# Three moves in the order of a codebook-convolution kernel: layer 3's bias product, the second chunk's weights, and the overflow count

## The chip, the cores and the metric

The kernel runs on one core of one Trainium2 chip. The metric is the device time of one execution in microseconds (us). The core has five engines that run their own instruction queues in order and wait for each other through semaphores: TensorE (PE in the profile; its weight loads are PEld), VectorE (DVE), ScalarE (ACT), GpSimd (POOL) and SyncE (SP), which here issues nearly all DMA transfers.

## The reference, cut to what matters

The input x is 32 images of 1024 channels and 14 x 14 pixels. Two blocks follow each other. The first one is a bottleneck of three "table" convolutions, each followed by a batch normalisation:

```python
def _amm(patches, centroids, lut, inv_temp):
    v = patches.reshape(B, ncb, sub, H * W).transpose(0, 3, 1, 2)
    scores = 2.0 * einsum('blcs,cks->blck', v, centroids) - sum(centroids * centroids, -1)
    attn = softmax(scores * inv_temp, axis=-1)
    out = einsum('blck,cko->blo', attn, lut)
    ...
out = relu(_bn(_amm(x, c1_centroids, c1_lut)))          # 1024 -> 256
out = relu(_bn(_amm(_extract3x3(out), c2_centroids, c2_lut)))  # 256 -> 256
out = _bn(_amm(out, c3_centroids, c3_lut))              # 256 -> 1024
x = x + relu(out + identity)
```

In words: the channels are cut into groups, each group of a pixel is scored against 16 centroids, a softmax over those 16 gives weights, and the output is the weighted sum of rows of a table. The second block is a linear attention with a depthwise convolution; the change doesn't touch it, and it is called stage 4 below.

## The kernel before, in words

**Stages.** The function `layers` runs the three table convolutions one after the other, then stage 4 follows. In a score product, 128 partitions hold 8 groups of 16 centroids. The softmax over 16 neighbours on the partition axis is done in five steps: ACT takes the exponentials out of PSUM (L568, with a bias for each centroid), DVE transposes in 32 x 32 blocks (L580, tile `tt`), POOL adds the two halves in layers 1 and 2 (L583), DVE sums and takes reciprocals (L599, L601) and transposes the reciprocals back (L611, tile `r`), and POOL multiplies (L618). Then SP spreads some rows to other partitions by small DMAs: where the last of the 16 weights would stand, the kernel puts a row of another tile (L713, L716 in layers 1 and 2; `spread3` and `double3`, L1139 to L1143, in layer 3), since the 16 weights add up to one.

**Layers 1 and 2** are run by `units`: 16 pairs of images times 8 blocks of channels are 128 units, numbered by i. In step i it issues the scores of unit i + 4, the first transpose of unit i + 3, the softmax of unit i + 2, the callback `side(i)`, and the table products of unit i (L734, "the products" below). `side2` is the callback of layer 2. At i = 60 it prepares layer 3: `score_biases` squares and sums the centroids on DVE into a scratch tile `croom`, which is taken from the same two-buffer pool and tag as `r`; `score_matrices` writes the score matrix `cw`; and then `biases()` multiplies on PE (L397, tile `pb`) and finishes on DVE (L401, L402, L406) into `cbias`.

**Layer 3** works on 14 chunks of 448 pixels, with two blocks of channels each, so that (k, b) names a softmax. The prologue does both of chunk 0 and the scores of (1, 0). `first_chunk` makes the eight outputs of chunk 0: outputs 0 to 2 together, then output 3, then 4 to 7 (`whole`, `halves`: L1275 in the profile; `out` copies by ACT at L1298 and takes statistics on DVE at L1257). Three PSUM banks plus one hold the outputs, so that output 4 needs the bank of output 0, and so on. `softmax_steps(k, b, t)` returns four steps: first transpose; sums; back (transpose, multiply, spread); and the sum for the overflow test, an ACT instruction (L622). Chunks 1 to 13 are made by `group(k, 0)` and `group(k, 1)`, which use a Strassen-like scheme with 7 products of halves instead of 8; it needs sums of table blocks (`weight_sums` on POOL, L1198 to L1200; `weight_differences` on DVE, L1206) and sums of softmax halves (`first_sum` on POOL, L1213; `other_sums` on DVE and POOL, L1219 to L1221). The products are at L1358.

**The overflow test.** Exponentials are taken without subtracting the maximum. `overflow` (L629 to L638) compares the sums with 1e36 on DVE (L632, L633), counts with a 1-column product on PE (L635), writes an integer (L637) and loads it into a register of all five engines (L638, `TENSOR_LOAD`). `layers` returns that register, and a branch at L1466 repeats the layers in an exact form if it is positive, which doesn't happen with these inputs. The test stands before the last chunk (k = 13).

**What sets the order.** Inside `layers` the schedule is written by hand: each engine runs its instructions in the order of the program. Only stage 4 has a planner.

Of the kernel before, what the change touches and what calls it, by code (L numbers as in the profile page):

```python
# [12 lines left out]
ALU = mybir.AluOpType  # L13
# [4 lines left out]
P = 128  # L18
# [131 lines left out]
def conv_preact_kernel(ctx: ExitStack, tc: tile.TileContext, a: dict, out: bass.AP):  # L150
    nc = tc.nc
# [347 lines left out]
    def layers(exact, early=None):  # L499
# [20 lines left out]
        parts = {}  # L520
# [35 lines left out]
        def scores(n):  # L556
            return ps_sc.tile([P, 512], F32, tag="sc", name="sc")[:, :n]
# [71 lines left out]
        def overflow(pool):  # L629

            good = pool.tile([P, 1], F32, tag="good", name="good")
            nc.vector.tensor_scalar(sums, sums, 1e36, None, ALU.is_le)  # L632
            nc.vector.tensor_reduce(good, sums, AX.X, ALU.min)  # L633
            pf = scores(1)[:1]
            nc.tensor.matmul(pf, good, ones[:, :1], start=True, stop=True)  # L635
            bad = pool.tile([1, 1], mybir.dt.int32, tag="bad", name="bad")
            nc.vector.tensor_scalar(bad, pf, -1.0, float(P), ALU.mult, ALU.add)  # L637
            return nc.values_load(bad[0:1, 0:1], min_val=0, max_val=P)  # L638

        def add_up(layer, n):  # L640
            if not exact:
# [318 lines left out]
        with ExitStack() as s:  # L960
# [77 lines left out]
            def side2(i):  # L1038

                for b in range(4, 8):  # L1040
                    if i == max(b - 7, -ahead):
                        luts2[b][2]()
                    if i == max(b - 4, 0):
                        luts2[b][4]()
                if i == max(-2, -ahead):
                    luts2[4][3]()
                p = {1: 1}.get(i + ahead, (i + ahead + 9) / 8)
                if p in range(1, NP):
                    for h in range(2):
                        store_pair(int(p), h)  # L1050
                if i == 60:
                    bias3, biases = score_biases(ps_tr, big, st, 3, raw[3], P, 2, mask8, 4)
                    parts[3] = score_matrices(big, 3, "", raw[3], mask8), bias3
                    biases()
                next_lut3(i - 8 * (NP - 1) - 1)

            def next_lut3(b):
# [25 lines left out]
        with ExitStack() as s:  # L1083
# [3 lines left out]
            again = None  # L1087
# [17 lines left out]
            def score3(k, b, parts=None):  # L1105
                v = chunk(k, b)
                scs = []
                for j in range(4):
                    sc = scores(NC)
                    r = slice(32 * j, 32 * j + 32)  # L1110
                    nc.tensor.matmul(
                        sc, w3[r, b, :], v[r], start=True, stop=True
                    )
                    scs.append(sc)
                t = sf.tile([P, 4, NC], F32, tag="t", name="t")
                if parts is None:
                    exponentials(t, scs, bias3[:, 4 * b : 4 * b + 4])
                    return t
                for v in (slice(0, 2), slice(2, 4)):
                    parts.append(  # L1120
                        lambda v=v: exponentials(
                            t[:, v], scs[v], bias3[:, 4 * b : 4 * b + 4][:, v]
                        )
                    )
                return t
# [67 lines left out]
            def weight_sums():  # L1193

                for g in range(3):
                    a11, a21 = luts[1 + g][:, :512], luts[1 + g][:, 512:]
                    a12, a22 = luts[4 + g][:, :512], luts[4 + g][:, 512:]
                    nc.gpsimd.tensor_tensor(s1[:, g], a21, a22, ALU.add)  # L1198
                    nc.gpsimd.tensor_tensor(s2[:, g], s1[:, g], a11, ALU.subtract)
                    nc.gpsimd.tensor_tensor(s4[:, g], a12, s2[:, g], ALU.subtract)  # L1200
# [7 lines left out]
            def first_sum(k):  # L1208
                x = sums3[k] = [
                    xs.tile([P, 3, H], F32, tag=f"x{n}", name=f"x{n}") for n in (1, 2, 4)  # L1210
                ]
                b1 = tiles3[k][0][:, 1:4]
                nc.gpsimd.tensor_tensor(x[0], b1[:, :, right], b1[:, :, left], ALU.subtract)  # L1213
# [9 lines left out]
            def softmax_steps(k, b, t):  # L1223


                u = 2 * k + b

                def spread():
                    tiles3.setdefault(k, []).append(t)
                    rows3[k] = rows3.get(k, []) + split3(t)  # L1230
                    spread3(rows3[k], range(4 * b + (b == 0), 4 * b + 4))
                    if b:
                        double3(rows3[k][0])

                if exact:

                    def whole():
                        softmax(st, u, t, *token_major(st, t))
                        spread()

                    return [whole] + 3 * [lambda: None]
                kept = {}

                def turn():
                    kept["t"] = token_major(st, t)

                def sums():
                    kept["back"], kept["total"] = softmax(st, u, t, *kept["t"], later=True)

                def back():  # L1250
                    kept["back"]()
                    spread()

                return [turn, sums, back, lambda: kept["total"]()]
# [9 lines left out]
            def first_chunk():  # L1264


                rows = rows3[0]
                pos = {}

                def bank(m):  # L1270
                    pool, tag = (ps_tr, "tr") if m % 4 == 3 else (ps_po, "po")
                    pos[m] = pool.tile([P, 512], F32, tag=tag, name="po3")[:, :NC]

                def product(m, g, r=slice(0, P), start=False, stop=False):
                    nc.tensor.matmul(  # L1275
                        pos[m],
                        luts[g][r, m * P : (m + 1) * P],
                        rows[g][r],
                        start=start,
                        stop=stop,  # L1280
                    )

                def whole(m):
                    for g in range(1, CT):
                        product(m, g, start=m == 4 and g == 1, stop=m > 4 and g == 7)

                def halves(m0):
                    for m in (m0, m0 + 1):
                        if m not in pos:
                            bank(m)  # L1290
                        r = slice(64 * (m - m0), 64 * (m - m0) + 64)
                        product(m, 0, r, start=m > 4, stop=m < 5)

                def out(m):
                    if m % 2 == 0:
                        pos["o"] = output()
                    o = pos["o"]
                    nc.scalar.copy(o[:, m % 2], pos[m])  # L1298
                    stats(m, o[:, m % 2], 0)
                    if m % 2:  # L1300
                        nc.sync.dma_start(o3d[:, m - 1 : m + 1, :NC], o)
                    if m in (4, 5):
                        relu3(2, m - 4)

                for m in range(3):
                    bank(m)
                for g in range(1, CT):
                    for m in range(3):
                        product(m, g, start=g == 1)
                bank(3)  # L1310
                for g in range(1, CT):
                    product(3, g, start=g == 1)
                halves(0)
                halves(2)
                out(0)
                for f in softmax_steps(1, 0, nxt):
                    f()
                first_sum(1)
                weight_sums()
                t = score3(1, 1)  # L1320
                out(1)
                bank(4)
                whole(4)
                halves(4)
                halves(6)
                for m in (2, 3):
                    out(m)
                for f in softmax_steps(1, 1, t):
                    f()
                out(4)  # L1330
                for m in range(5, 8):
                    whole(m)
                    if m == 7:
                        weight_differences()
                        other_sums(1)
                    out(m)

            first_chunk()
# [106 lines left out]
                pending.extend(steps[3:])  # L1445

            for k in range(1, NCH):
                if k + 1 == NCH and not exact:
                    add_up(2, 2 * NCH)
                    again = overflow(once)  # L1450
                if early:
                    early.pop(0)(scores)
                for n in range(2):
                    group(k, n)
            bn_final(once, None, 3, range(CT), sc3, bi3, mv3)
        act.close()
        return again
# [802 lines left out]
```

## Time and profile before

| what | value |
|---|---|
| time, median of 3 runs (lowest to highest) | 3439.27 us (3438.05 to 3441.15) |
| the profiled execution's own time | 3446.09 us |
| its span, first to last instruction | 3444.3 us |
| busy share PE / DVE / POOL / ACT | 98% / 85% / 74% / 49% |
| mean granted TensorE clock | 0.990 |
| layer 2's products run from 867 to 1641 us | L734, second half |
| first chunk of layer 3 | 1659.7 to 1709 us |
| groups (1, 0) to (13, 1) | 1709 to 2291 us |
| stage 4 | 2299 us to the end |

A line of a timeline gives start, duration, engine, source line, operation and tile, and in brackets how long the engine had been idle before it and what ended that. A float32 product appears as two matmuls. The granted clock is the share of full speed that TensorE was given in a window. Idle time of an engine that isn't the limit costs nothing.

### The profile page before, as it was taken

What the parts mean: (1) busy time and instruction counts of PE and PEld (TensorE: products, weight loads), DVE (VectorE), ACT (ScalarE), POOL (GpSimd) and SP (SyncE); (2) the same over time, 40 slices, a digit from 0 to 9 for tenths busy, and PEclk for the clock granted to TensorE, in tenths of its full rate; (3) what the DMA queues carried; (4) which work ended last, traced back from release to release, by engine and by line L of the source; (5) the groups of instructions that cost most, each with busy time, mean ns of one, the idle gap of its engine ahead of it and who ended that gap; (6) DMA issues with size and microseconds to landing.
All of it is one profiled execution on the core that took longest, in us unless ns stands there. A gap on an engine that the chain in (4) does not pass through costs nothing. (4 is left out here: it accounts for less than half of the span.)

```text
span 3444.3 us, 54933 instructions
## 1 busy us (share of the span) xinstructions
PE 3368.4 (98%) x19217; PEld 2088.5 (61%) x19217; DVE 2938.9 (85%) x4621; ACT 1671.0 (49%) x3843; POOL 2538.4 (74%) x1558
## 2 busy tenths in 40 slices
PE   8999999998999999999999999979999999999999
PEld 4555555554455445545488888866666666666665
DVE  7999999997888888888576666646999999999996
ACT  4555555554444434443311111118676767676765
POOL 5999999996888988898322222218888888888887
PEclk9999999999999999999999999989999999999999
DMA  3110111103434444443131111131233332333221
GB/s 117 46 48 28 46 46 47 30 24 113 134 109 128 123 114 109 127 123 98 33 91 38 49 49 49 47 130 41 69 90 87 87 87 81 87 87 91 79 76 48
DMA packets 242229, 267.44 MB, mean 78 GB/s; under 512 B 32812, under 2 KB 239700, under 8 KB 241944
## 3 DMA queue, kind: packets, MB, share of 16 engines
q1 hardware_dynamic: 241248, 263.52, 26.3%
q8 instruction: 155, 2.54, 0.3%
q14 instruction: 130, 1.06, 0.1%
q10 hardware_dynamic: 696, 0.31, 0.0%
HBM read 171.01 MB, written 77.09 MB: 72 GB/s over the span
## 5 line engine op out<-in xcount | busy, mean ns | idle before, releaser
L618 POOL TENSOR_TENSOR t<-t,r 128x1568 f32<-128x1568 f32 (+3 forms) x288 | 961.5, 3339 | 531.5 <-issue 201.1
L734 PE MATMUL po<-t,lut 128*128 128x392 f32 x3840 | 1334.6, 500 | 2.5 <-DMA t<-spare 2.5
L734 PEld LDWEIGHTS po<-t,lut 128*128 128x128 f32 x3840 | 711.9, 190 | 603.8 <-issue 83.2
L1770 PE MATMUL mm<-y,lut 128*128 128x392 f32 x2048 | 710.4, 493 | 0.1
L580 DVE STREAM_TRANSPOSE tt<-t 128x1568 f32<-128x1568 f32 (+1 forms) x284 | 517.8, 1823 | 153.4 <-ACT t L568 149.1
L568 ACT ACTIVATE t<-sc,cbias 128x392 f32<-128x392 f32 (+1 forms) x624 | 322.4, 598 | 554.5 <-PE sc L897 191.2
L1992 DVE SCALAR_TENSOR_TENSOR pa<-y,lepe_w,pa 128x406 f32<-128x406 f32 x900 | 537.9, 638 | 3.6 <-PE pa L1974 0.3
L611 DVE STREAM_TRANSPOSE r<-rc 128x1568 f32<-128x1568 f32 (+1 forms) x284 | 520.9, 1834 | 10.4
L1770 PEld LDWEIGHTS mm<-y,lut 128*128 128x128 f32 x2048 | 370.4, 188 | 243.1 <-issue 6.1
L583 POOL TENSOR_TENSOR tt<-tt 128x784 f32<-128x784 f32 x256 | 470.6, 1838 | 30.5 <-DVE tt L580 25.9
L568 ACT ACTIVATE t<-sc,room 128x392 f32<-128x392 f32 x512 | 259.1, 589 | 410.2 <-issue 180.1
L1358 PE MATMUL po<-t,lut 128*128 128x224 f32 (+2 forms) x1352 | 314.8, 416 | 1.3 <-DMA o3d<-o 1.3
L599 DVE TENSOR_REDUCE sm<-tt 128x98 f32<-128x784 f32 (+1 forms) x284 | 293.6, 1034 | 1.1 <-POOL tt L583 0.8
L1358 PEld LDWEIGHTS po<-t,lut 128*128 128x128 f32 (+1 forms) x1352 | 234.7, 190 | 64.5 <-issue 61.8
L601 DVE RECIPROCAL rc<-sm 128x98 f32<-128x98 f32 (+1 forms) x284 | 220.2, 775 | 9.8
L622 ACT ACTIVATE sm<-sm 128x98 f32<-128x98 f32 (+1 forms) x284 | 85.5, 301 | 150.5 <-DVE rc L601 150.5
L1623 ACT ACTIVATE w<-x,tb,gn_a 128x196 f32<-128x196 f32 x248 | 128.3, 517 | 53.8 <-DMA qr<-o3d 29.3
L1814 POOL TENSOR_TENSOR kr<-k,cosq 128x784 f32<-128x784 f32 x64 | 104.3, 1629 | 63.5 <-DVE k L1791 36.7
L1955 POOL TENSOR_TENSOR qr<-qr,zb 128x784 f32<-128x784 f32 x64 | 117.9, 1854 | 39.2 <-DMA zb<-zd 31.5
L1779 ACT ACTIVATE e<-mm,kbd 128x392 f32<-128x392 f32 x128 | 74.5, 582 | 145.4 <-PE mm L1770 145.4
L1782 ACT ACTIVATE e<-e 128x392 f32<-128x392 f32 x256 | 134.9, 527 | 2.1
L1736 ACT ACTIVATE y<-x,gb,ga 128x196 f32<-128x196 f32 x256 | 125.3, 544 | 12.1 <-POOL gb L1699 12.1
(215 smaller groups left out, 4613.1 us busy)
## 6 DMA issues: line engine op xcount, KB each, us to landing
patch<-h1d SPq DMA_DIRECT2D x383, 108.5 KB
x<-in_x_dram SPq DMA_DIRECT2D x32, 784.0 KB
o3d<-o SPq DMA_DIRECT2D x56, 448.0 KB
x<-in_x_dram SPq DMA_DIRECT2D x64, 392.0 KB
out_dram<-x SPq DMA_DIRECT2D x64, 392.0 KB
o<-o3d SPq DMA_DIRECT2D x62, 392.0 KB
h1d<-pad SPq DMA_DIRECT2D x96, 225.0 KB
patch<-h1d SPq DMA_DIRECT2D x383, 54.2 KB
```

Of the source, the lines that this page charges most:

```text
L568: nc.scalar.activation(t[:, j, : sc.shape[1]], sc, AF.Identity if exact else AF.Exp, bias=bias[:, j : j + 1],)
L580: nc.vector.transpose(tt, tf)
L583: nc.gpsimd.tensor_tensor(tv[:, :, :8], tv[:, :, :8], tv[:, :, 8:], ALU.add)
L599: nc.vector.tensor_reduce(sm, tv, AX.X, ALU.add)
L601: nc.vector.reciprocal(rc, sm)
L611: nc.vector.transpose(r, bc(rc, 2, KC))
L618: nc.gpsimd.tensor_tensor(v[:, c], v[:, c], r[:, c], ALU.mult)
L734: nc.tensor.matmul(po[h], luts[b][:, j, h * P : (h + 1) * P], ts[u % len(ts)][:, j, :N2], start=(b == 0 and j == j0), stop=(b == 7 and j = ...
L1358: nc.tensor.matmul(dst, w, x, start=start, stop=stop)
L1770: nc.tensor.matmul(pv(), w[kt][:, m0 : m0 + P], ywin(p, first + kt), start=(kt == 0), stop=(kt == 3),)
L1782: nc.scalar.activation(e(), e(), AF.Exp, scale=-1.0)
L1992: nc.vector.scalar_tensor_tensor(acc, neighbours(p, c, offset(k)), lw[:, c, k : k + 1], acc, ALU.mult, ALU.add,)
```

## The change

Three moves; no arithmetic is added or removed.

1. `biases()` of layer 3 is called four units later, at i = 64, while the DVE work on its operands stays at i = 60. The scratch tile `croom` is therefore held four units longer.
2. In `first_chunk`, the softmax of (1, 0) and `first_sum(1)` are issued at the start; the scores of (1, 1) go between the products of outputs 0 to 2 and those of output 3; the softmax of (1, 1) and then `weight_sums` follow ahead of the first `out`; and `other_sums(1)` moves ahead of `out(4)`.
3. `overflow` returns a function. The comparison stays ahead of the last chunk; the count on PE and the integer on DVE come behind `group(13, 0)`, and the register loads behind `group(13, 1)`, which is ahead of the final normalisation `bn_final`.

```diff
+            def count():
+                pf = scores(1)[:1]
+                nc.tensor.matmul(pf, good, ones[:, :1], start=True, stop=True)
+                bad = pool.tile([1, 1], mybir.dt.int32, tag="bad", name="bad")
+                nc.vector.tensor_scalar(bad, pf, -1.0, float(P), ALU.mult, ALU.add)
+                return lambda: nc.values_load(bad[0:1, 0:1], min_val=0, max_val=P)
+
+            return count
...
                     parts[3] = score_matrices(big, 3, "", raw[3], mask8), bias3
-                    biases()
+                    parts["biases3"] = biases
+                if i == 64:
+                    parts["biases3"]()
...
                 for m in range(3):
                     bank(m)
+                for f in softmax_steps(1, 0, nxt):
+                    f()
+                first_sum(1)
                 for g in range(1, CT):
                     for m in range(3):
                         product(m, g, start=g == 1)
+                t = score3(1, 1)
                 bank(3)
                 for g in range(1, CT):
                     product(3, g, start=g == 1)
+                for f in softmax_steps(1, 1, t):
+                    f()
+                weight_sums()
                 halves(0)
                 halves(2)
                 out(0)
-                for f in softmax_steps(1, 0, nxt):
-                    f()
-                first_sum(1)
-                weight_sums()
-                t = score3(1, 1)
                 out(1)
...
                 for m in (2, 3):
                     out(m)
-                for f in softmax_steps(1, 1, t):
-                    f()
+                other_sums(1)
                 out(4)
...
                         weight_differences()
-                        other_sums(1)
...
             for k in range(1, NCH):
+                check = None
                 if k + 1 == NCH and not exact:
                     add_up(2, 2 * NCH)
-                    again = overflow(once)
+                    check = overflow(once)
                 if early:
                     early.pop(0)(scores)
-                for n in range(2):
-                    group(k, n)
+                group(k, 0)
+                if check:
+                    check = check()
+                group(k, 1)
+                if check:
+                    again = check()
```

More of the change, by code (lines that the diff above doesn't have):

```diff
@@ L633, in overflow @@
             nc.vector.tensor_reduce(good, sums, AX.X, ALU.min)
[L634 to L638, printed above, removed]
+            def count():
[5 more added lines that the diff above has]
+            return count
         def add_up(layer, n):
```

## The prediction

> **What bounds the kernel now.** First the page's busy shares:
>
> ```profile
> PE 3368.4 (98%) x19217; PEld 2088.5 (61%) x19217; DVE 2938.9 (85%) x4621; ACT 1671.0 (49%) x3843; POOL 2538.4 (74%) x1558
> ```
>
> PE is the limit, so only PE's gaps and slow stretches are worth anything. The second view is the waits of PE, asked for the three places that the change touches:
>
> ```profile
> PE po L1358 <- DVE x L1219: 5.6, 1, 5.6
> PE pb L397 <- DMA patch<-h1d: 5.5, 1, 5.5
> ...
> PE sc L635 <- DVE good L633: 2.3, 1, 2.3
> ...
> PE po L1358 <- DMA o3d<-o: 1.3, 1, 1.3
> ...
> PE po L1275 <- ACT o L1298: 1.1, 1, 1.1
> ```
>
> They sum to 15.8 us. The row of L397 names a DMA, but the timeline shows whom PE waited for: L397 needs DVE's L388 (1234.63, 0.29 long), which stood behind an L344 of 3.18 us. The products of unit 60 then began at 1235.56.
>
> ```profile
> 1230.80 3.49 POOL L618 TENSOR_TENSOR t<-t,r 128x1568 f32<-128x1568 f32 x1 [1.00 <-ACT t L568]
> ...
> 1231.13 3.18 DVE L344 TENSOR_SCALAR cmean3b<-cmean3b,cinvt3b 128x2 f32<-128x2 f32 x1
> ...
> 1234.98 0.79 PE L397 MATMUL pb<-croom 128*128 128x128 f32 x2 [5.53 <-DMA patch<-h1d]
> ```
>
> The third view, busy time in three stretches (PE, weight loads, DVE, ACT, POOL, then granted clock, DMA share, GB/s), shows what a gap costs afterwards: the granted clock is 0.51 to 0.64 after each long gap.
>
> ```profile
> 1235.00:1242.00 7.00, 7.00 (x30) 3.86 (x46) 6.69 (x11) 0.00 (x0) 1.83 (x1) 0.64 0.48 129
> 1720.30:1724.80 4.50, 4.46 (x12) 4.06 (x13) 4.48 (x3) 0.00 (x0) 1.45 (x1) 0.51 0.60 207
> 2247.40:2251.20 3.80, 3.80 (x13) 3.54 (x14) 0.00 (x0) 0.35 (x1) 0.00 (x0) 0.61 0.00 0
> ```
>
> **Move 1, the bias product.** Score groups, one a unit (L1027), follow each other by 6.34 us (1215.83, 1222.17, 1228.51), by 5.00 where a unit has 12 products instead of 16 (1204.49 to 1209.49). Unit 60 has 12, so the scores behind 1228.51 were due at 1233.51; they came at 1241.83: 8.3 us lost, 6.2 waiting and 2.1 at half clock. The matmul itself still runs at i = 64: 0.4 (from 1234.97 to the next weight load at 1235.35).
>
> Where does the stall go? DVE still spends 1230.6 to 1236.0 on L382 to L356; only L401, L402 and L406 (0.29 + 0.29 + 0.17) leave. So DVE's next transpose (L580, unit 64) starts at 1236.0, though its input was there at 1231.7 (L568 from 1229.64, 2.02 long): DVE is 4.3 us late. How much lead is there? Unit 61's multiply ends at 1228.01, its small DMA is issued by 1228.64 and lands some 1.4 later (the same DMA of 1236.45 moved its bytes until 1238.4), at 1230.0; undisturbed, its products would start at 1234.4. Lead 4.4 against lateness 4.3: a knife edge. DVE catches up slowly, because `croom` keeps one of the two buffers of `r`: each L611 must now wait for the L618 before it. That hand-over is 1.81 + 0.1 + 3.52 + 0.1 = 5.6 us against a mean unit of (3 x 6.34 + 5.00)/4 = 6.0. Followed through by these rows, operands reach PE at 1247.0 for unit 63 (due 1247.1), 1252.8 for 64 (1253.8), 1258.2 for 65 (1258.8), 1263.8 for 66 (1265.1).
>
> Then a rule enters. L406 now falls at about 1260, within a POOL multiply (1258.4 to 1261.9); before, POOL was idle and it took 0.17. [...] The L344 above is that case: it ended at 1234.31, POOL's L618 at 1234.29, and its twin took 0.23 without POOL. By L406's own row (0.17) unit 67 is about 0.5 us early and nothing is lost; by the rule L406 takes 2.0, unit 67's operands land at 1272.9 against 1271.5, and PE loses 1.4. The L344 rows decide for me: I take 1.5 (between 0 and 3.5, the longest multiply). Gain 8.3 - 0.4 - 1.5 = **6.4** (4.4 to 7.9).
>
> **Move 2, the first chunk.** Here POOL multiplied (1, 1) only at 1712.36, behind nine weight sums; the spread landed at 1719.4:
>
> ```profile
> 1712.33 2.43 PE L1358 MATMUL po<-x,s 128*128 128x224 f32 x12
> 1712.36 3.97 POOL L618 TENSOR_TENSOR t<-t,r 128x1792 f32<-128x1792 f32 x1
> ...
> 1719.43 0.86 DVE L1219 TENSOR_TENSOR x<-t,x 128x672 f32<-128x672 f32 x1 [9.50 <-DMA t<-t]
> ...
> 1720.34 4.68 PE L1358 MATMUL po<-x,s 128*128 128x224 f32 x12 [5.58 <-DVE x L1219]
> ```
>
> The new order, by the same rows. DVE, idle from 1662.1, does (1, 0): 2.03 + 2.02 + 0.85 + 2.04, until 1669.2; POOL multiplies until 1673.3, SP spreads, `first_sum` ends at 1678.3. PE makes 21 products at 0.75 (1659.7 to 1675.5), then the (1, 1) scores; ACT's exponentials run 1677.0 to 1679.2, DVE until 1686.3, POOL until 1690.4; the spread (landing 3.1 behind its first issue, as at 1716.36 to 1719.43) is there at 1693.5, x2 and x4 by about 1696, the nine sums (1.3 each) by 1702, or 1705 if they are held at 1.7 each, as when L1206 ran. Group (1, 0) wants the sums from 1711.8 and x2 at 1714.4: everything is early, and the 5.6 us and the half clock behind it (12 matmuls in 4.3 against 2.3 for the twelve before them: 2.0) go.
>
> What is queued behind? On ACT, `out(0)` now stands behind the overflow sum of (1, 1), which waits for the reciprocals (1684.3). So `out(0)` copies until 1685.4, and output 4 needs its bank: PE, free at 1684.1, waits 1.4. The additional change of row count costs 0.46 (weight loads at 1680.11 and 1680.95, instead of a pitch of 0.375). Against this, the present 2.2 us stall in `halves` disappears (1689.08 to 1693.01 is 3.93; the same work took 1.71 at 1680.95). Together 0.3 gained. On SP the first two output stores slip behind the spreads to about 1697; their buffers are reused at 1711. The thirteen loads for stage 4 begin at about 1710 rather than 1722.6 and last 12, still ahead of the spread of (2, 0), some 20 us into the group. On DVE x2's wait for the spread now stands ahead of the statistics of output 4, which come later than 1693.5 anyway. POOL's queue ends with L1220 after the sums, at 1704 to 1707; its result is wanted some 11 us into the group. Gain **7.9** (6.5 to 9.6: no wait for `out(0)` at the top).
>
> **Move 3, the overflow count.** PE's row behind the count:
>
> ```profile
> 2247.38 3.98 PE L1358 MATMUL po<-t,lut 128*128 128x224 f32 x12 [1.34 <-DMA o3d<-o]
> ```
>
> and, from the rows of one line (minimum, median and maximum duration in ns, then first and last start):
>
> ```profile
> L638 DVEq TENSOR_LOAD <-bad x1: 750/750/750, 2246.5 to 2246.5; - x1
> ```
>
> PE finished group (12, 1) at 2243.6; the second set of group (13, 0) began at 2251.19: 7.6 us for work that takes 2.4 in group (12, 0) (2200.76 to 2203.14). So 5.2 are lost: a gap of 3.8 and 1.4 of half clock. (The wait named a DMA is the register load: 0.75 from 2246.4.) Afterwards the count costs PE two changes of shape (0.46 each, nearest row) and its passes, 1.1 (0.2 to 1.5). `bad` on DVE finds the count done. The loads wait for semaphore values long reached; ACT, POOL and PE have slack there, and SP's stores come first. On DVE the load stands between the last statistics (end 2293.5) and `bn_final`, which stage 4 waits for: 0.75 if nothing overlaps plus 0.3 for its five waits, less what overlaps with the statistics' 0.53; I take 0.6 (0 to 1.1). Gain 5.2 - 1.1 - 0.6 = **3.5** (2.6 to 5.0).
>
> **The sum.** 6.4 + 7.9 + 3.5 = 17.8 us. From the profiled execution's 3446.09 (span 3444.3 and 1.8 around it) that gives 3428.3; from the median of the runs, 3439.27, it gives **3421.5**.
>
> **The rivals.**
> - *The stall comes back elsewhere.* The knife edge in layer 2 and ACT's `out(0)` are both covers of about 0; if both miss by 3 to 4 us (a gap of 3.8 has already cooled the clock, one of 1.1 at 1690 left it at 1.00), 8 of the 17.8 return: 3429. For it: one buffer of `r`, and ACT's strict order. Against: the rows above have each link early or at zero.
> - *Every cover holds.* L406 isn't held, `out(0)` comes in time, the load overlaps: 17.8 + 1.5 + 1.4 + 0.6 = 21.3: 3418.
> - *It doesn't do what it says.* If x2 is as late as now, because the nine sums on POOL (two SBUF inputs) and DVE's x2 and x4 (also two) shut each other out far longer than at 1719 to 1722 (2.14 and 2.29 instead of 0.86 and 1.6), and layer 2 stalls again in full, only move 3 remains: 3436.
> - *Slower.* The single `r` buffer chains DVE and POOL over five units. At 5.6 us per hand-over it recovers; from 6.0 it accumulates, and it outweighs all gains (19.3 with move 1's gross) and 0.2% when each of the five is 5.2 later, at 11 us: about 3447. No row is near 11.
>
> **How the numbers follow.** 0.2% of the time, 6.9 us, is about what a measurement tells from no change. Likeliest case 0.61 (3418 to 3426), stall back 0.20, every cover 0.12, not doing it 0.04, slower 0.03. Faster by over 0.2% (below 3432.4): 0.61 + 0.12 + 0.17 of the second = 0.90; within: 0.07; slower 0.03. The range from 3415 (all upper ends: 22.5 gained, 3416.8, and the runs' 1.5) to 3430 leaves out the worst third of the stall's return and the last two cases, under 2 in 10.
>
> **What would show it.** In layer 2 no gap ahead of L397 and a clock of 1.00 at 1229 to 1242; L406 at about 2 us; a wait of PE at L734 for a DMA about five units later, of 0 to 3 us. In layer 3 L1219 at about 1694 less the earlier gain, a wait of PE for ACT's L1298 of about 1.4, none at L1358 for DVE. Between groups (12, 1) and (13, 0) no gap; a short one around the count; `bve` (L318) some 0.6 later behind the statistics than now. The forecast is wrong if a PE wait over 3 us stands in layer 2 near unit 63 to 67, or if the clock falls again in one of the three places.

## The result

| | before | after |
|---|---|---|
| time, median (lowest to highest, 4 runs each) | 3439.22 us (3438.05 to 3441.15) | 3418.64 us (3417.50 to 3422.85) |
| profiled execution, its span | 3446.09, 3444.3 us | 3419.37, 3417.6 us |
| mean granted TensorE clock | 0.990 | 0.995 |

The ratio is 0.9942 (95% interval 0.9925 to 0.9959): 20.6 us by the medians, where the forecast said 17.8 (3421.5, range 3415 to 3430). The page of the changed kernel, busy shares:

```profile
PE 3356.3 (98%) x19217; PEld 2081.5 (61%) x19217; DVE 2938.2 (86%) x4621; ACT 1672.1 (49%) x3843; POOL 2535.9 (74%) x1558
```

Among PE's waits the rows for the bias product of layer 3 (L397), for x2 and for the overflow count are gone. Three of the rows that the changed kernel has:

```profile
PE mm L1666 <- DVE tb L1502: 10.1, 1, 10.1
...
PE po L738 <- DMA t<-spare: 4.8, 4, 1.6
...
PE po L1281 <- ACT o L1304: 1.0, 1, 1.0
```

The same three places by busy time (columns as before the change) have PE busy all through and a clock of 1.00, where the kernel before had 0.64, 0.51 and 0.61:

```profile
1224.00:1236.00 12.00, 12.00 (x124) 5.70 (x112) 11.62 (x18) 4.69 (x12) 6.49 (x3) 1.00 0.69 203
1699.71:1704.20 4.49, 4.49 (x28) 4.49 (x25) 1.95 (x2) 2.81 (x6) 0.00 (x0) 1.00 0.60 143
2227.40:2231.20 3.80, 3.80 (x22) 3.80 (x21) 0.21 (x2) 0.35 (x1) 0.00 (x0) 1.00 0.45 168
```

To see where the time came from, the span was cut at the starts of PE's own products: layer 2's first score, the scores of unit 64 (the last group of matmuls ahead of the old stall), those of unit 100, the first product of the first chunk, of group (1, 0), of (12, 0), of (13, 0), the last product of layer 3, and the first of stage 4. Lengths in us, from the profiled executions; each kernel has 2600 group products and 7022 matmuls in stage 4, so the marks are the same work:

| stretch | before | after | move 1 alone | move 2 alone | move 3 alone |
|---|---|---|---|---|---|
| start to layer 2 | 839.5 | 835.2 | 839.9 | 834.4 | 834.1 |
| to the scores of unit 64 | 389.0 | 388.7 | 389.0 | 389.7 | 389.9 |
| to the scores of unit 100 | 224.57 | 219.90 | **219.84** | 224.78 | 224.69 |
| to the first chunk | 206.63 | 206.63 | 206.64 | 206.64 | 206.63 |
| first chunk | 50.25 | 49.33 | 50.25 | **49.33** | 50.24 |
| groups (1, 0) to (11, 1) | 490.8 | 482.8 | 493.0 | **482.8** | 490.9 |
| groups (12, 0), (12, 1) | 46.61 | 42.66 | 46.65 | 46.64 | **42.66** |
| groups (13, 0), (13, 1) | 42.77 | 41.54 | 43.86 | 43.88 | **41.54** |
| to stage 4's first product | 11.82 | 10.67 | 12.29 | 12.06 | 12.88 |
| stage 4 | 1142.3 | 1140.1 | 1140.4 | 1140.5 | 1146.8 |

The row "to the first chunk", which nothing in the change touches, repeats to 0.01 us (206.63); the start, 834 to 840, scatters by itself and is no part of the gain. In the changed kernel move 1 gave 4.7, move 2 0.9 + 8.0 = 8.9, and move 3 3.95 + 1.2 = 5.2 in its groups. Two rows didn't fit: the way to stage 4 became 1.15 shorter, although the register load had been put there, and stage 4 itself isn't constant. These are what the experiments had to settle, besides the sizes of the three terms.

### The profile page after: what moved, and what is told of

The parts are those of the page before. It is cut to its first block, busy times and chain, and to the rows that moved or that the text cites. A ratio compares the mean times of both kernels' runs of the same rounds, so it can differ in the third digit from the quotient of the medians.

```text
span 3417.6 us, 54936 instructions
## 1 busy us (share of the span) xinstructions
PE 3356.3 (98%) x19217; PEld 2081.5 (61%) x19217; DVE 2938.2 (86%) x4621; ACT 1672.1 (49%) x3843; POOL 2535.9 (74%) x1558
## 3 DMA queue, kind: packets, MB, share of 16 engines
q14 instruction: 129, 1.06, 0.1%
## 5 line engine op out<-in xcount | busy, mean ns | idle before, releaser
L611 DVE STREAM_TRANSPOSE r<-rc 128x1568 f32<-128x1568 f32 (+1 forms) x284 | 520.8, 1834 | 11.6 <-POOL t L618 1.2
L1031 PE MATMUL sc<-patch,room 27*32 27x392 f32 x4096 | 123.1, 507 | 8.6 <-DMA patch<-h1d 8.6
```

The costliest lines, as they stand in the source:

```text
L611: nc.vector.transpose(r, bc(rc, 2, KC))
```

## The experiments

### The three moves alone

Each kernel is the kernel before with one of the three parts of the diff, nothing else.

> Move 1 alone, the rest as before. By the forecast's term 6.4 us faster than the kernel before (8.3 gross, 0.4 for the matmul itself, 1.5 of stall five units later). By the trace of the full change 4.7 us (8.3 - 0.4 - 3.2 of waits for the spare rows at units 63, 67 and 70). If moves don't add, because the stall in layer 2 only pushes a wait into layer 3's beginning, the times of the three single moves will sum to clearly more or less than the 20.6 us of the whole change. The theory of additive terms: 4.7 for this one, with waits of PE at L738's line for the spare of 1.1, 0.4 and 1.6; the sums of the three single moves 18 to 21.

> Move 2 alone. By the forecast's term 7.9 us faster than before, by the trace of the full change 9.2 (one wait of 1.0 for ACT's copy of output 0 in place of 5.6 at x2 and the half clock behind it). Rival: part of the 9.2 is owed to move 1 (loads for stage 4 or the table rows come at another moment), then this kernel gains 6 or less and waits at x2 again.

> Move 3 alone. By the forecast's term 3.5 us faster, by the trace of the full change 4.0 (5.2 gross, 0.3 for the count, 0.85 for the register load on DVE). Rival: the 2 to 3 us by which the whole change gained more than its three terms come from here, through stage 4's start (the first DVE instruction behind the branch ran 2 us earlier in the changed kernel): then 6 to 7 us faster, and the gap on DVE between the last instruction of the final normalisation and the first of stage 4 is 3.3 us instead of 5.3. If it is scatter of that gap from execution to execution, the gap differs between kernels that have the same move or lack it.

Measured beside the kernel before (3447.6 us in this comparison): move 1 3435.1, ratio 0.9964 (0.9951 to 0.9978); move 2 3432.6, 0.9955 (0.9942 to 0.9969); move 3 3443.0, 0.9986 (0.9979 to 0.9993). That is 12.5, 15.0 and 4.6 us: the gains of moves 1 and 2 alone exceed what the whole change gave. By the stretches above they don't: each move shortens its own rows (in bold) by what it shortens there in the full change, and no other of the five. One of them is uncertain: groups (13, 0) and (13, 1) took 42.8 us in the kernel before and 43.9 with move 1 or move 2 alone, so that move 3's part there is 1.2 or 2.3. With that reserve the terms add (the rival of a wait pushed elsewhere falls), and the excess sits in something the kernels compared did not have in common. Stage 4 shows it: 1140 to 1142 us in four of the five profiles, 1146.8 with move 3 alone.

PE's waits with move 1 alone and then with move 2 alone, between 1200 and 1300 us and between 1660 and 1740 us:

```profile
PE po L734 <- DMA t<-spare: 3.1, 3, 1.5
```

```profile
PE po L1275 <- ACT o L1298: 1.0, 1, 1.0
```

### A build that isn't the same twice

Stage 4's planner goes through its engines as a Python set of their names, and the order of such a set is drawn anew for every process. The sequence of PE's products in stage 4, read from the traces, came in two forms: one in the profiles of before, after, move 1 and move 2, the other in move 3 alone and the own-tile kernel below; at 1444 of the 7022 places a product of another source line stands. Building the changed kernel with the order written out, for 24 different orders, gave the first form in each of the 12 with POOL ahead of DVE, and the second in the 12 with DVE ahead of POOL. So this was fixed:

```diff
-        engines = {p[0] for p in self.pieces}
+        engines = ("PE", "POOL", "DVE", "ACT", "SP")
```

> The kernel before, with one line changed: stage 4's planner walks over its five engines in a fixed order (PE, POOL, DVE, ACT, SP) instead of over a Python set of their names, whose order is drawn anew each time the program is built. The traces so far show two orders of PE's products in stage 4: one in the profiles of the kernel before, of the changed one, of move 1 alone and of move 2 alone (1140.1 to 1142.3 us from stage 4's first product to the end), the other in move 3 alone and in the own scratch tile (1146.8 and 1146.8). The fixed order gives the first. If the build's order is what made the kernel before take 3447.6 us in the last comparison, against 3439.2 at first, this kernel takes about 6.5 us less than the unpinned one where that has the second order, and the same (within 1.5) where it has the first: 3439 to 3441 either way. Rival: the chip is slower by 8 us, then this one stands at 3447.

> The changed kernel with the same fixed order in the planner. The difference to the pinned kernel before is the change alone: by the single moves' stages 4.75 (layer 2) + 0.9 and 8.0 (first chunk and the half clock after it) + 4.0 and 1.2 to 2.3 (overflow count, the gap and the half clock) - 0.8 (register load), 18 to 19 us; by the forecast's terms 17.8; by the medians of the first comparison 20.6. If stage 4's first DVE instruction is again ahead of POOL's memsets by luck, 2 more.

Measured: the pinned kernel before 3440.8 us, beside the unpinned one at 3447.2 (ratio 0.9982, 0.9975 to 0.9988); stage 4 1142.2. The pinned changed kernel took 3420.3 (ratio to the unpinned kernel before 0.9920, 0.9907 to 0.9934), again 3420.3 in a later comparison; stage 4 1139.5 and 1140.1. The 6.4 us between the two builds of one source are of the size of the gap between the two forms' stage 4: 1138.5 to 1142.3 in the twelve profiles of the first form, 1146.8 in both of the second. That the unpinned kernel before was of the second form in these later comparisons is inferred from this; no profile of it was taken there. In the first comparison both profiles have the first form, so the 20.6 us there are free of it, and the pinned pair gives 20.5. Against the pinned kernel before, moves 1 and 2 alone gain 5.7 and 8.2; move 3, which has the second form, gains 4.6 against the unpinned one: together 18.5. The change as a whole gains 20.5, so 2.0 were still without an owner. The intervals of these gains are some us wide each; that the 2.0 are more than scatter is shown only by the traces, below.

### The own scratch tile

```diff
-        room = tmp.tile([P, 4 * N2], F32, tag="r", name=f"croom{i}")[:rows]
+        if i == 3:
+            room, a1, a2 = spare_room[0].rearrange("p g k -> p (g k)"), 32, 160
+        else:
+            room, a1, a2 = tmp.tile([P, 4 * N2], F32, tag="r", name=f"croom{i}")[:rows], 512, 1024
```

Here `spare_room` is layer 2's raw centroids, which are done with by then.

> The changed kernel, with the scratch of layer 3's bias in a tile of its own, so that the softmax tile r has both buffers throughout. If the single buffer costs time, the added waits of DVE's back-transpose for POOL (0.33, 0.50, 0.36 us at units 63 to 66) go and PE's waits for the spare rows fall from 3.2 to about 2.0 (1 us faster). Rival: POOL itself has 5.4 us of work a unit, as much as the chain over the single buffer (5.6), so the buffer costs under 0.3 us and the waits stay at 3.2.

The one execution took 3428.2 us, with stage 4 in its second form. The stretch from unit 64 to 100 took 218.98 us, 0.9 less than 219.90, and PE's waits there fell from 3.2 (first fence, changed kernel) to 2.3 (second, own tile):

```profile
PE po L738 <- DMA t<-spare: 3.2, 3, 1.6
```

```profile
PE po L743 <- DMA t<-spare: 2.3, 3, 1.5
```

The single buffer of `r` cost 0.9: with it DVE's back-transposes (L611) of units 63 to 66 follow each other by 5.5 to 5.7 us, with the own tile by 5.2. The larger part of the stall is something else, and the same kernel's timeline points to it: its last bias addition, 128 x 8 elements, is held even longer.

```profile
1251.98 3.52 POOL L623 TENSOR_TENSOR t<-t,r 128x1568 f32<-128x1568 f32 x1
...
1252.91 2.62 DVE L409 TENSOR_SCALAR cbias<-cb 128x8 f32<-128x8 f32 x1
```

### Six edits at once, and the three that stand outside layer 2

Besides the own tile: `score_matrices` moved from i = 60 to 62; the last bias addition reads PSUM; and three edits at other places:

```diff
-                for f in softmax_steps(1, 1, t):
+                steps = softmax_steps(1, 1, t)
+                for f in steps[:3]:
                     f()
                 weight_sums()
...
                 out(1)
+                steps[3]()
...
         pow_mhalf(sc[:, v], ve)
+        value = load() if load else None
...
+                if k == 0:
+                    nc.gpsimd.tensor_copy(t[:, :1, :1], tb[:, :1, :1])
```

The second hunk is in `bn_final`, which is handed the function with the register load; the last puts POOL's memsets of stage 4 behind `tb`, stage 4's first DVE instruction.

> The changed kernel (fixed order in the planner) with six further edits: the bias scratch of layer 3 in a tile of its own; the score matrix of layer 3 made at unit 62 instead of 60; the bias's last addition reading PSUM instead of SBUF; the overflow sum of softmax (1, 1) issued behind the copies of outputs 0 and 1; the register load behind the power function of the last normalisation, where DVE waits for POOL; and the memsets of stage 4 on POOL behind the first DVE instruction of stage 4. By the trace's terms: 3.2 in layer 2, 0.9 in the first chunk, 0.85 and 2.1 at the start of stage 4, together 7 us under the pinned changed kernel (5 if that one is lucky with the memsets). Rivals: the score matrix at unit 62 meets a POOL multiply again and part of the 3.2 stays; the load on POOL or PE becomes the last thing ahead of the branch and the 0.85 stays.

> The changed kernel (fixed order in the planner) with only the three edits outside layer 2: the overflow sum of (1, 1) behind outputs 0 and 1, the register load behind the power function, the memsets behind stage 4's first DVE instruction. Expected in the trace: no wait of PE for ACT's copy of output 0 and the first chunk 0.9 to 1.0 shorter (49.3 to 48.4); from the last product of layer 3 to the first of stage 4 12.9 - 0.85 - 2.1 = 9.9 us. Rival for the load: 10.8 (it only moves its time to the branch). Rival for the memsets: what held DVE was not POOL but the arrival of its code behind the branch, then 12.0.

All six: 3418.1 us (ratio 0.9914, 0.9901 to 0.9928), 2.3 under the pinned changed kernel instead of 5 to 7, which the scatter of five executions each doesn't tell surely from nothing. The three outside layer 2: one execution of 3418.2. The stretches say more:

- The first chunk took 48.22 us in both, 1.1 less than 49.33, and PE no longer waits for ACT there: confirmed.
- The way to stage 4 took 9.78 us with the three edits, against 10.7 in the changed kernel: the load, 0.54 long on DVE now and under the 1.66 of POOL's power function, gave its 0.95 back. In the kernel with all six it took 12.00.
- That 12.00 is the rival's number for the memsets, and they fall as a cause. In this kernel POOL comes behind `tb`, and `tb` was just as late (gap 5.47):

```profile
2278.78 0.43 DVE L1517 TENSOR_TENSOR tb<-gn_b,bi 128x256 f32<-128x256 f32 x1 [5.47 <-issue]
2279.27 0.18 POOL L1525 COPY y<-tb 128x1 f32<-128x1 f32 x1 [6.56 <-DMA qr<-o3d]
```

- Layer 2 gained nothing (219.78, with 1.5 to 2.7 more than in the other profiles ahead of unit 64). The moved score matrix was held, twice, by the two multiplies of one unit (1.11 and 2.63):

```profile
1242.78 1.11 DVE L346 TENSOR_SCALAR cmean<-cmean,cinvt 128x2 f32<-128x2 f32 x1
1242.82 1.04 POOL L626 TENSOR_TENSOR spare<-t,r 128x392 f32<-128x392 f32 x1
1243.81 2.71 POOL L631 TENSOR_TENSOR t<-t,r 128x1176 f32<-128x1176 f32 x1
1243.93 2.63 DVE L347 SCALAR_TENSOR_TENSOR craw<-craw,cinvt,cmean 128x32 f32<-128x32 f32 x1
```

At i = 60 these two had stood behind an instruction held already, and took 0.23 and 0.25. Moving them bought a second hold. So moving the small steps doesn't help by itself. The next pair of kernels moves their operands instead.

### The small steps with operands in PSUM

Only the own tile, and each small step with at most one operand in SBUF; the two `tensor_scalar` that had been held, which read one tile of SBUF each, now read theirs in PSUM:

```diff
+                    pm = ps_tr.tile([P, 512], F32, tag="tr", name="pm")
...
-        centre(pool, i, "b", sq, -1.0)
+            v, sq = sq, ps[:, : groups * KC].rearrange("p (g k) -> p g k", k=KC)
+            centre(pool, i, "b", v, -1.0, ps[:, 32:34], sq)
...
+            src, raw = raw, ps[:, 64:96].rearrange("p (g k) -> p g k", k=KC)
+            centre(pool, i, name, src, 2.0, ps[:, 34:36], raw)
...
+                b3 = pbt[:, 512 - n :]
+                nc.vector.tensor_reduce(b3, pv, AX.X, ALU.add)
+                nc.vector.tensor_scalar(bias, b3, -SHIFT, None, ALU.add)
```

`ps` is `pm`, a tile in PSUM; the mean, the centred values and the sums now lie there.

> The changed kernel (fixed order in the planner), with the bias scratch of layer 3 in a tile of its own, and the small DVE steps of layer 3's bias and score matrix at units 60 and 64 rewritten so that each reads at most one operand from SBUF, with its mean, its centred values or its sums in PSUM. The theory: [...] (3.21 us for a mean of 128 x 2 elements, 2.21 for the last addition), so neither is held any longer, DVE is 2.2 us late instead of 5.4 behind unit 60, less than the lead of 4.4, and all three waits of PE for the spare rows go: the stretch from the scores of unit 64 to those of unit 100 takes 216.7 us instead of 219.9. Rival: the first step of the chain [...], or any PSUM one, is held just as long (as one of 2.6 was in the combined kernel), and the stretch stays between 218.5 and 219.9.

> The same, with the overflow sum of (1, 1) behind the copies of outputs 0 and 1 and the register load behind the power function. If the theory of the run before holds: 3.1 in layer 2, 1.1 in the first chunk and 0.95 at the end of layer 3, 5.2 us under the changed kernel with the fixed order (3420.3), 3415; 2.1 more, 3417, if the code of DVE behind the branch comes late in this build, as it does in seven of the ten kernels so far. A memset of POOL is not moved. Whether the gap comes is told by DVE's records ahead of the branch: with 2577 of them none, with 2572, 2573 or 2576 one of 2.1 to 2.3 us.

The stretch took 216.49 us in both kernels, 0.2 under the forecast of 216.7, and PE has no wait left between 1200 and 1300 us. The first of the two, whose one execution took 3417.4 us, has this timeline; POOL's multiply runs from 1225.32 to 1228.84, and the last line has another beside it (1249.35 to 1252.88):

```profile
1225.32 3.52 POOL L638 TENSOR_TENSOR t<-t,r 128x1568 f32<-128x1568 f32 x1 [0.98 <-ACT t L588]
1225.66 0.23 DVE L345 TENSOR_SCALAR pm<-pm,cinvt3b 128x2 f32<-128x2 f32 x1
1225.92 0.26 DVE L346 SCALAR_TENSOR_TENSOR pm<-craw,cinvt3b,pm 128x32 f32<-128x32 f32 x1
...
1250.70 0.17 DVE L418 TENSOR_SCALAR cbias<-pb 128x8 f32<-128x8 f32 x1
```

The mean that took 3.21 takes 0.23 and the addition that took 2.21 takes 0.17, with POOL at work in both. With the two edits at the first chunk and the load as well: 3416.95 us (ratio 0.9917, 0.9903 to 0.9930), and a way to stage 4 of 11.87, so the late `tb` was back.

### DVE's code behind the branch

In the traces, DVE's first instruction behind the branch ahead of stage 4 comes 2.8 to 3.1 us after the branch, in all 14 profiles. Then either everything up to `tb` follows within 0.6 us, or DVE stands still for 2.0 to 2.3 us more between two instructions at a place that differs: one, three or four instructions behind the branch's target. What goes with it is the number of DVE's records ahead of the branch. Profiles with 2577 of them (after, its pinned builds, the three edits) have no such gap; profiles with 2572 (before and its pinned build, move 3, own tile, six edits, and the two with PSUM operands), 2573 (move 2) or 2576 (move 1) have it. Hence the last pair of kernels, the first being the one above (3416.95) with:

```diff
     nc.vector.memset(ones, 1.0)
+    for _ in range(5):
+        nc.vector.memset(ones, 1.0)
```

> The kernel of the last timed run with five more tiny memsets on DVE at the very start, where DVE idles; they write the ones that are there already. In that run DVE stood still for 2.15 us behind the branch ahead of stage 4, three instructions past the branch's target, with 2572 of DVE's records ahead of it; no wait of it and no work of POOL ends there. If it is the next piece of DVE's program that comes late, [...] 2577 records, no gap, as in the three kernels that had 2577, and 9.7 us instead of 11.9 from layer 3's last product to stage 4's first: 2.1 us faster. Rival: the gap belongs to something that DVE waits for, and five memsets 2270 us earlier change nothing.

> The changed kernel with the fixed order in the planner once more, for a comparison on the same chip: 3420.3 (3418.6 in the first comparison), with 2577 records and no gap of DVE behind the branch, as in its other two builds. The kernel beside it should be 5 us faster: 3.3 in layer 2, 1.1 in the first chunk, 0.95 for the register load, within the scatter of the start-up and of single clock dips of about 2 us.

2577 records, and no gap: 9.89 us to stage 4 instead of 11.87. The line of `tb` without the five memsets:

```profile
2272.93 0.43 DVE L1525 TENSOR_TENSOR tb<-gn_b,bi 128x256 f32<-128x256 f32 x1 [5.33 <-POOL y L1539]
```

And with them:

```profile
2271.17 0.42 DVE L1527 TENSOR_TENSOR tb<-gn_b,bi 128x256 f32<-128x256 f32 x1 [3.37 <-DVEq L1502]
```

Five instructions, 2270 us earlier, take 2 us away: what counts is the number of instructions ahead of the branch, not a wait for work. The releaser "POOL y" in the first fence (and in the kernel before) is only the last event that happened to precede. The DMA records that the traces mark as instruction transfers fit: in each of the 14 profiles one such packet starts about 1.0 us after DVE's branch (1.03 in the kernel before, 1.04 in the changed one) and another 3.4 to 3.7 us after it (3.50 and 3.49). DVE's first instruction runs just under 2 us after the first of them starts (in these two 2.93 and 2.88 us after the branch), and where DVE stands still again, it goes on 1.7 to 1.9 us after the second (in the kernel before 5.24 us after the branch). That these packets carry DVE's code is inferred from the times.

In time the padded kernel took 3417.7 us (3413.5 to 3419.5) beside 3420.3 for the changed kernel, ratios to the kernel before of 0.9913 (0.9898 to 0.9928) and 0.9923 (0.9909 to 0.9936). By the stretches of the two profiles it is 5.2 us shorter (219.75 - 216.49, 49.32 - 48.22 and 10.69 - 9.89); but two of its four executions took 3419.4 and 3419.5 at a mean clock of 0.993 and 0.992, the other two 3413.5 and 3416.0 at 0.995. The medians' 2.6 us is thus a gain that these runs do not tell surely from the scatter, though its parts are seen one by one in the traces. It is the shortest span of all (3411.7 us).

## Why the prediction was right, and where it was not

The time fell inside the range, 2.9 us under the forecast, because the three gross terms were right to a few tenths: 8.3 us in layer 2, 5.6 and the cool clock behind it at x2 (7.6 in all, measured 8.0), 5.2 at the count. Each move's net gain (4.7, 8.9 and 4.3) lies in the range given for it. What the moves cost, and one gain that the sum did not have, are another matter.

**Move 1: 4.7 instead of 6.4, the stall behind it 3.2 instead of 1.5.** The step that was mis-sized is "I take 1.5 (between 0 and 3.5)". What led up to it happened. The line of L406 before, and then the timeline of the changed kernel:

```profile
1236.66 0.17 DVE L406 TENSOR_SCALAR cbias<-cb 128x8 f32<-128x8 f32 x1
```

```profile
1226.47 3.21 DVE L344 TENSOR_SCALAR cmean3b<-cmean3b,cinvt3b 128x2 f32<-128x2 f32 x1
...
1243.62 5.50 PE L738 MATMUL po<-t,lut 128*128 128x392 f32 x16 [1.14 <-DMA t<-spare]
...
1249.93 0.49 PE L397 MATMUL pb<-croom 128*128 128x128 f32 x2
...
1253.55 3.52 POOL L618 TENSOR_TENSOR t<-t,r 128x1568 f32<-128x1568 f32 x1 [0.18 <-issue]
...
1254.89 2.21 DVE L406 TENSOR_SCALAR cbias<-cb 128x8 f32<-128x8 f32 x1
...
1268.35 3.86 PE L738 MATMUL po<-t,lut 128*128 128x392 f32 x11 [0.43 <-DMA t<-spare]
```

The matmul cost its 0.4, and L406 was held for 2.21. The forecast had 0.17 for it by its own old row, and 2.0 if it is held to the end of POOL's multiply, as the L344 of the kernel before was (3.18 beside POOL, 0.23 without). The measurement sides with the hold: L406 ended at 1257.10, POOL's multiply at 1257.07. Up to unit 67 the 1.5 was right: unit 63 made PE wait 1.14 and unit 67 another 0.43, 1.57 together, and unit 67's operands came at 1268.35, where the sum's 1272.9, moved to this kernel's time, is 1268.2. In its parts the sum was off, since it had unit 63 ready 0.1 before it was due. (Its multiply ended when the sum said, but the last notice of its spread's landing came 3.06 us after the issue, the one before it at 2.17. Why, no run shows. Had it come in time, unit 67 would by the same reckoning have waited the longer.) But there the forecast stopped, and unit 70 made PE wait another 1.60. That wait comes through a queue that the sum had not followed, SP's. The changed kernel again:

```profile
1277.42 0.61 SPq L717 DMA_DIRECT2D t<-spare  x1
...
1278.13 2.91 SPq L983 DMA_DIRECT2D h1d<-pad  x6
...
1278.45 3.54 POOL L618 TENSOR_TENSOR t<-t,r 128x1568 f32<-128x1568 f32 x1
...
1281.17 4.06 SPq L1001 DMA_DIRECT2D patch<-h1d  x6
...
1285.33 0.61 SPq L717 DMA_DIRECT2D t<-spare  x1
...
1287.80 4.52 PE L738 MATMUL po<-t,lut 128*128 128x392 f32 x13 [1.60 <-DMA t<-spare]
```

Unit 69's late spread (1277.42) lets SP go on to six stores and six patch loads, and unit 70's spread, whose multiply ended at 1281.99, leaves only at 1285.33. The kernels with PSUM operands show what the whole lateness cost: 219.90 - 216.49 = 3.4 us, of which the single buffer of `r` is 0.9 and the two holds the rest. (By the prediction's own terms that buffer's hand-over sums to 5.5 us, not 5.6.) In the kernel with six edits a `scalar_tensor_tensor` with two inputs in SBUF was held as well: 2.63 us beside POOL's multiply, against 0.25 with POOL idle (kernel before, at 1235.38). With one of the two in PSUM it took 0.26 beside POOL.

**Move 2: 8.9 instead of 7.9.** PE's wait for `out(0)` was there, 1.0 instead of 1.4, with the first chunk shorter by 0.9 instead of 0.3, and x2 was ready long before it was wanted (at 1683.94; the sum's 1693.5, moved to this kernel's time, is 1684.2):

```profile
1675.60 23.22 PE L1281 MATMUL po<-t,lut 128*128 128x448 f32 x64 [1.04 <-ACT o L1304]
1683.94 1.59 DVE L1225 TENSOR_TENSOR x<-t,x 128x672 f32<-128x672 f32 x1 [5.06 <-DMA t<-t]
1702.09 4.70 PE L1364 MATMUL po<-x,s 128*128 128x224 f32 x24
```

The gap and the half clock behind it were worth 8.0, against 7.6 in the sum. That the wait came from ACT's order is shown by taking it away: with the overflow sum issued behind the copies PE doesn't wait, and the chunk is another 1.1 us shorter.

**Move 3: 5.2 in the groups, less 0.95 for the load, 4.3 instead of 3.5.** The step that was mis-sized is the count's 1.1. The two matmuls stand between the groups,

```profile
2246.09 0.19 PE L637 MATMUL sc<-ones,good 128*1 128x1 f32 x2
```

and the lead over the kernel before is 23.72 us ahead of them (second set of products of (13, 0), 2251.19 to 2227.47) and 23.40 behind them (of (13, 1), 2271.99 to 2248.59): 0.3, near the low end of what was allowed. One group earlier, with nothing between, this stretch takes the changed kernel 20.80 us, as it does the kernel before at this place; with the count it takes 21.12. The load cost DVE 0.9 instead of 0.6 (moving it under the power function returned 0.95), so it did not overlap the statistics:

```profile
2270.98 0.17 DVE L318 TENSOR_SCALAR bve<-mv 128x8 f32<-128x8 f32 x1 [0.88 <-DMA o3d<-o]
```

**What no step held: 2.0 us.** The sum by its own steps, with the measured sizes, is 4.7 + 8.9 + 4.3 = 17.9; that this is the 17.8 of the forecast is luck, since move 1's -1.7, move 2's +1.0 and move 3's +0.8 cancel. The medians differ by 20.6. Of the 2.7 between, 2.0 is DVE's gap behind the branch: the changed kernel's `tb` came 3.29 us after DVE's last instruction instead of 5.28 (first fence, before). The 0.7 left is within the scatter of the runs. Stage 4 could hold some of it: it took 1142.3 and 1142.2 us in the two profiles of the kernel before and 1138.5 to 1141.0 in the other ten of its form, and why stays open.

```profile
2301.33 0.42 DVE L1491 TENSOR_TENSOR tb<-gn_b,bi 128x256 f32<-128x256 f32 x1 [5.28 <-POOL y L1505]
```

```profile
2276.78 0.43 DVE L1502 TENSOR_TENSOR tb<-gn_b,bi 128x256 f32<-128x256 f32 x1 [3.29 <-DVEq L1477]
```

It is not owed to what any move does but to how many instructions they leave ahead of the branch: with 2577 of DVE's records there was no gap, with 2572, 2573 or 2576 one of 2.0 to 2.3 us. That DVE waits for its code in it is inferred from the times of the instruction transfers alone; why the number decides, no run shows.

**The rivals.** "The stall comes back elsewhere" happened in part: waits of 3.2 us in layer 2 and 1.0 for `out(0)`, of which the forecast had 1.5 and 1.4, not 8 on top. "Every cover holds" had the right time (3418) for a wrong reason: none of its three covers held, and the gap that is gone behind the branch (2.0) and move 2's other gains made up for most of them. "Slower by the single buffer" had the right mechanism at 0.9 us.

## What to carry to other kernels

A move that takes a wait off the path keeps its gross gain only if what it makes late has slack; when lead and lateness come out equal, follow the lateness until the late engine has caught up, unit by unit, through every queue that serves it, and count every hold on the way. Here a small DVE step beside a busy POOL waited for the rest of POOL's instruction in two cases: a `scalar_tensor_tensor` with two inputs in SBUF (2.63 us), for which it was enough to put one of them in PSUM (0.26); and a `tensor_scalar`, which was held with a single tile of SBUF to read (L344 3.21, L406 2.21) and was not with that tile in PSUM (0.23 and 0.17). Before two builds are compared to a fraction of a per cent, see that they are the same program outside the edit: here the order of a Python set was worth 6.4 us, more than move 1 or move 3, and five tiny instructions ahead of a branch 2.0.

## What the runs showed of the hardware that was not expected

- DVE's stall behind the branch has two parts: 2.8 to 3.1 us in all 14 profiles, and in nine of them 2.0 to 2.3 us more, one to four instructions behind the target; five more instructions ahead of the branch removed the second part (3.37 us to `tb` instead of 5.33).
- A `tensor_scalar` of 128 x 2 elements took 3.21 us and a `scalar_tensor_tensor` of 128 x 32 took 2.63 beside POOL multiplies; with PSUM operands, 0.23 and 0.26 beside such a multiply.
- The register load took from 0.49 us (PE) to 1.06 us (SP) in the changed kernel; on DVE it took 0.85 there, and 0.54 issued under POOL's power function.
- In some executions the clock falls without a long gap of PE, at about 1832 us, and the groups take 1.7 us more (484.5 instead of 482.8). PE idles 0.76 us in the 4 us ahead of it. The own-tile kernel had the fall in its profile; the changed kernel, with the same 0.76, kept a clock of 1.00:

```profile
1832.00:1836.00 4.00, 4.00 (x14) 3.69 (x14) 1.41 (x1) 1.76 (x4) 0.00 (x0) 0.62 0.00 0
```

What decides it stays open. It is as large as the effect of a single edit, so differences of this size between times of one execution each tell nothing.
